# Two attention layers on one core: when normalizations start, how the divisors travel, and where the division stands

## The chip, the core and the metric

The kernel runs on one core of a Trainium2 chip. A time is the device time of one execution in microseconds (us); lower is better. The core has five engines that each work through their own queue in order: PE (TensorE, matrix products into PSUM), DVE (VectorE), ACT (ScalarE), POOL (GpSimd) and SP (SyncE, which here only issues transfers). An engine that waits at the head of its queue holds up everything behind it.

## The reference

The input `x` is 4 images of 256 channels and 64 x 64 pixels, in float32. Two layers follow, each with a residual:

```
x = x + layer0(group_norm(x))
x = x + layer1(group_norm(x))

layer0: q = Wq x                              (8 heads of 32 channels, 4096 queries)
        k, v = convolutions 2x2, stride 2     (1024 keys and values)
        out = softmax((q k + q pos) / sqrt(32)) v
layer1: q, k, v = 1x1 convolutions
        attention within each of 4 areas of 1024 pixels
        out = W_proj (attention + depthwise convolution 7x7 of v)
```

A group norm takes the mean and the variance over 8 channels and all pixels of an image, so its scale is known only when the whole image has been seen. Everything is computed in float32.

## The kernel before

**Units.** The attention of both layers and four images makes 128 units: 4 heads and 512 queries against 1024 keys. A unit has 8 steps, one for each 128 keys. Layer 0 of all four images comes first (`A`, batches 0 to 3), then layer 1 (`B`).

**Phases.** A main loop (L1157) runs 683 phases, each of one and a half steps. In a phase PE computes scores for three PSUM banks (`scores`, L430, products at L423), ACT takes three exponentials of them, 128 x 1024 each (L464 and L475, tile `p` or, in the first step of a unit, `acc`), PE multiplies the exponentials of the phase before by the values (`weighted`, L489, into the bank `av`), and DVE adds the exponentials up in `acc` (`add_up`, L499). The loop writes the order of every engine's queue by hand; nothing is reordered later.

**Side work.** Everything else is fitted into the phases. `at(g, j, f)` runs `f` after step `j` of unit `g`. `task_at` puts generator tasks (projections, convolutions) into the queue `side`; each phase takes 0, 1, 2 or, when late, 4 parts of it, if the task's `ready` allows. Only one PSUM bank is there for side work (`ps_side`). A phase does one of three things (L1181 to L1209): a unit's divisors, an entry of the queue `quick`, or parts of `side`.

**Normalization.** `plan_norm` (L331) plans three pieces for each image and layer: `aggregate` (DVE), then `means` and `variances`, both put into `quick`. `means` multiplies by the group matrix on PE (L347), copies on ACT (L348) and lets DVE form the deviation (L349 to L351); `variances` multiplies again (L355), ACT adds epsilon (L356), POOL takes the power -1/2 (L359) and forms the shift (L363, L364). Only then `norms[key]` is set. `later` (L282) queues the normalizations themselves (ACT, L387, on the loaded tiles `taps`, `hq`, `h`, `hv`), each with the earliest phase at which it may run: some phases after its load was issued. `norm_next` (L290) takes the first that is due at the end of a phase. `normalize` (L378) has a way out when the scale isn't there:

```
while key not in norms:
    while begun():
        advance()
    quick.popleft()()
```

**Division.** When a unit's sums are complete, `divisors` (L501) lets PE sum `acc` over the keys by products with ones (L508, bank `den`), and `divide` (L513) does the rest. Each head's 512 divisors stand in 32 equal partitions of `den`. ACT copies them to `den_sb` (L522). POOL sends 4 rows of it to the DRAM tile `rows` (L523) and from there, spread over 128 partitions as 128 x 16, into `few` (L524). A unit later DVE takes reciprocals of that small tile and sums for a check (`reciprocals`, L530, L531), POOL sends them to the DRAM tile `recs` (L532) and by four broadcasts into `rb` (L534, 32 partitions each, one buffer). Some steps later `multiply` (L537) on DVE multiplies `av_sb` by `rb` into `att`. `av_sb` is ACT's copy of the bank `av` (`evict`, L1118, L1124) and has two buffers. Steps of the two, for unit `g`:

```
at(*((g + 2, 1) if g < len(units) - 2 else (g + 1, 6)), reciprocals)
at(g + 2, 6 if g < len(units) - 2 else 0, multiply)
```

**What reads the result.** The residual of a chunk is added at (u + 2c + 4, 1) after its two units (L670, L813); the tile `att` has one buffer.

Of the kernel before, what the change touches and what calls it, by code (L numbers as in the profile page):

```python
# [9 lines left out]
FP = mybir.dt.float32  # L10
# [5 lines left out]
P = 128  # L16
# [44 lines left out]
def direct_path(  # L61
# [127 lines left out]

    side, quick = deque(), deque()
    now, last = [-1], len(BLOCKS) * UNITS * NKT

    phase = [0]
# [76 lines left out]
    def begun():  # L272
        return bool(side) and side[0][2]

    norms_left, norm_done = [], {}

    copies, behind = [0], [0.0]

# [10 lines left out]

    def norm_next(token=None):  # L290
        for n, (of, f, start) in enumerate(norms_left):
            if (of == token) if token else start <= phase[0]:
                del norms_left[n]
                f()
                norm_done[of] = phase[0]
                return True
        return False
# [33 lines left out]
    def plan_norm(key, g, j):  # L331

        name = f"{key[0]}{key[1]}"
        made = {}

        def aggregate():
            for tag, cols in (("mv", 2), ("gmean", 1), ("dev", 1), ("gvar", 1)):
                shape = [P, CT, cols] if cols > 1 else [P, CT]
                made[tag] = pool.tile(shape, FP, tag=tag, name=f"{tag}_{name}", bufs=2)
            mv = made["mv"]  # L340
            for t in range(CT):
                V.bn_aggr(out=mv[:, t, :], in_=stats[key][:, t].rearrange("p c s -> p (c s)"))

        def means():
            mv, mean, dev = made["mv"], made["gmean"], made["dev"]
            ps = ps_side(f"gm_{name}")[:, :CT]
            T.matmul(ps, lhsT=gmat, rhs=mv[:, :, 0], start=True, stop=True)  # L347
            S.copy(mean, ps)  # L348
            V.tensor_sub(dev, mv[:, :, 0], mean)  # L349
            V.tensor_mul(dev, dev, dev)  # L350
            V.tensor_add(dev, dev, mv[:, :, 1])  # L351

        def variances():
            ps = ps_side(f"gv_{name}")[:, :CT]
            T.matmul(ps, lhsT=gmat, rhs=made["dev"], start=True, stop=True)  # L355
            S.activation(made["gvar"], ps, AF.Identity, bias=eps)  # L356
            norm = pool.tile([P, 2, CT], FP, tag="norm", name=f"norm_{name}", bufs=8)
            shift, rstd = norm[:, 0, :], norm[:, 1, :]
            G.tensor_tensor(rstd, made["gvar"], neghalf, ALU.pow)  # L359
            if key == ("A", 0):  # L360
                V.scalar_tensor_tensor(shift, made["gmean"], -1.0, rstd, ALU.mult, ALU.mult)
            else:
                G.tensor_tensor(shift, made["gmean"], rstd, ALU.mult)  # L363
                G.tensor_scalar(shift, shift, -1.0, None, ALU.mult)  # L364
            norms[key] = shift, rstd

        def quietly(f, n):
            f()
            if key == ("A", 0):
                keep_busy(n)  # L370

        if key == ("A", 0):
            at(g - 1, 0, lambda: keep_busy(44))
        at(g, j, aggregate)
        at(g, j + 1, lambda: soon(lambda: quietly(means, 4)))
        at(g, j + (6 if g >= 0 else 3), lambda: soon(lambda: quietly(variances, 10)))
# [136 lines left out]
    def divide(g, unit):  # L513

        if g == len(units) - 1:

            V.tensor_mul(unit[4]()[:, unit[0], :], avs.pop(g), spare[1])  # L517
            return
        den_sb = pool.tile([P, CH], FP, tag="cout", name="den_sb", bufs=2)
        few = pool.tile([P, 2, CH // HD], FP, tag="few", name="few", bufs=2)  # L520
        rows = dram.tile([4, CH], FP, tag="rows", name=f"rows_{g}", bufs=4)
        S.copy(den_sb, dens.pop(g))  # L522
        G.dma_start(rows, den_sb[0:P:HD, :])  # L523
        G.dma_start(few[:, 0, :], rows.rearrange("h (q n) -> (h q) n", n=CH // HD))  # L524
        made = {}

        def reciprocals():
            rb = made["rb"] = pool.tile([P, CH], FP, tag="rb", name="rb", bufs=1)
            recs = dram.tile([4, CH], FP, tag="recs", name=f"recs_{g}", bufs=4)
            V.reciprocal(few[:, 1, :], few[:, 0, :])  # L530
            V.tensor_reduce(sums[:, :, g], few, AX.X, ALU.add)  # L531
            G.dma_start(recs.rearrange("h (q n) -> (h q) n", n=CH // HD), few[:, 1, :])  # L532
            for h in range(4):
                G.dma_start(rb[HD * h : HD * h + HD, :], recs[h : h + 1, :].to_broadcast([HD, CH]))  # L534

        def multiply():
            V.tensor_mul(unit[4]()[:, unit[0], :], avs.pop(g), made["rb"])  # L537

        at(*((g + 2, 1) if g < len(units) - 2 else (g + 1, 6)), reciprocals)
        at(g + 2, 6 if g < len(units) - 2 else 0, multiply)  # L540

    def att_of(key):
        if key not in atts:
# [4 lines left out]
    def plan_a(b, u, prep):  # L548
# [78 lines left out]
        for a in range(NAREA):  # L627
            g = prep + (1 + 3.6 * a if b == 1 else 0.05 + 3.7 * a if b else 6 + 2.2 * a)
            at(0, int(NKT * (g - 2.4)), lambda a=a: load(a))
            for n in range(8):  # L630
                at(0, (max(int(NKT * (g - 1.9)), 3) if b else int(NKT * (g - 1.6))) + n, lambda a=a, n=n: later(("taps", b, a), lambda: make_taps(a, n), fetched["a", a] + 4))
            for n in range(2):
                if b == 0 and a and n:
                    held.append((4, make_k, a, n))
                else:
                    task_at(int(NKT * (g + 0.6 * n)), 4, make_k, a, n, due=min(g + 3.7, u) if a < 3 or not n else u + 0.3, ready=normed("taps", b, a))
                task_at(
                    int(NKT * (g + 0.6 * n + 1.2)), 4, make_v, a, n, due=min(g + 4.2, u - 0.2), ready=normed("taps", b, a)
                )
# [38 lines left out]
        for c in range(NCH):  # L678
            g = u + 2 * c
            at(g - 3, 4, lambda c=c: fetch(c))  # L680
            for t in range(CT):
                at(g - 2, 1 + 2 * t, lambda c=c, t=t: later(
                    ("hq", b, c), lambda: norm_chunk(c, t), fetched["q", c] + 5, True
                ))
            for qd in range(2):
                task_at(NKT * (g - 2) + 4, 2, make_q, c, qd, due=g - 0.3, ready=normed("hq", b, c))
            at(g + 3, 0, lambda c=c: load_residual(c))
            at(g + 4, 1, lambda c=c: add_residual(c))
            at(g + 4, 2, lambda c=c: store_chunk(c))
# [12 lines left out]
    def plan_b(b, u):  # L702
# [67 lines left out]
        for a in range(NAREA):  # L770
            g = u + 4 * a
            at(g - 6, 3, lambda a=a: load(a))
            for t in range(CT):
                at(g - 5, 2 + 3 * t, lambda a=a, t=t: later(("hs", b, a), lambda: norm(a, t), since[a] + 6, True))
            for n in range(4):
                task_at(
                    NKT * (g - 4) + 1 + 4 * n, 2, make_k, a, n // 2, n % 2, due=g - 0.4, ready=normed("hs", b, a)
                )
            for n in range(4):
                at(g - 4, 3 + 2 * n, lambda a=a, n=n: load_v(a, n))  # L780
                at(g - 2, 1 + 2 * n, lambda a=a, n=n: make_v(a, n))
# [161 lines left out]
    def plan_values(b, c, start):  # L943
# [46 lines left out]
        when = int(start * NKT)  # L990
        at(0, when - 5, load)
        for t in range(CT):
            at(0, when + 5 + t, lambda t=t: later(("hv", b, c), lambda: norm(t), made["at"] + 6, True))
        for t in range(CT):
            task_at(
                when + 7, 2, values, t, due=start + 4,
# [160 lines left out]
    while f < PHASES or before or plan or side or quick or norms_left or to_add or to_divide:  # L1157
# [27 lines left out]
        elif due and not begun():  # L1185
            done_den = 1
            copies[0] += 1
            g = to_divide.popleft()
            divisors(g, *([last - 1] if g == final else []))
            if g < final:  # L1190
                divide(g, units[g])
            else:
                rb = pool.tile([P, CH], FP, tag="p", name="rb", bufs=PB)
                V.reciprocal(rb, dens[g])  # L1194
                spare.extend((dens.pop(g), rb))
        elif quick and not begun() and not cut and f < PHASES:
            quick.popleft()()
        else:
            if rate > 2:
                parts = side_parts(4)  # L1200
            elif rate > 1.5 or due or f >= PHASES or wanted >= (0.8 if cut else 1.5):
                parts = side_parts(2)
            elif begun() and side[0][0] % 2:
                parts = side_parts(1)
            elif boundary(mine):
                parts = side_parts(2) if wanted >= 0.9 else 0
            elif wanted >= 0.5 and not cut or begun():
                parts = side_parts(1)
            credit = max(-0.5, min(wanted - parts, 0.5))  # L1209
# [620 lines left out]
```

## Time and profile before

| what | us |
|---|---|
| median of 3 runs | 3091.56 (3090.89 to 3096.43) |
| the profiled execution | 3092.91 |
| its span, from the first to the last instruction | 3090.8 |
| VectorE busy in sums of exponentials (L499) | 2113.9, 1790 of 1218 ns |
| ScalarE busy in exponentials of 128 x 1024 (L464, L475) | 2033.8, 2048 of about 1.03 us |
| POOL issuing transfers of divisors (L523, L524, L532, L534) | 467.7 |
| mean granted TensorE clock | 0.996 |

Times in the profile belong to the one profiled execution. "Busy" is time in which an instruction runs on the engine; a line of the waits view has who waited, for whom, the total in us, how many times, and the longest. A line of a timeline has start, duration, engine, line of the code, operation, tile written and tiles read, shape, count of merged instructions and, in brackets, how long the engine stood idle before it and what ended that. A line of the windows view has a stretch of time and its length, then for each engine its busy time, and at the end the granted TensorE clock, the share of the DMA engines and GB/s.

### The profile page before, as it was taken

The numbers are of one execution on the slowest core, as the hardware profiler recorded it, in microseconds if no ns is written. First come the engines' busy times: TensorE is split into PE (matmuls) and PEld (weight loads), VectorE is DVE, ScalarE is ACT, GpSimd is POOL, SyncE is SP. The second block draws the span as 40 slices with busy tenths as digits, with TensorE's granted clock in tenths as the row PEclk, the third lists the DMA queues.
The fourth block names the chain that finished last, engine by engine and source line by source line (L and its number), as shares of the span: only waits on it lengthen the run. The fifth ranks groups of instructions, "written<-read, shape, count | busy, mean of one in ns | idle before, by whom it ended". The sixth has DMA issues, their size and how long they took to land. (4 is left out here: it accounts for less than half of the span.)

```text
span 3090.8 us, 108514 instructions
## 1 busy us (share of the span) xinstructions
PE 3036.6 (98%) x47254; PEld 1282.2 (41%) x47254; DVE 2516.2 (81%) x2721; ACT 2455.2 (79%) x2988; POOL 483.1 (16%) x921
## 2 busy tenths in 40 slices
PE   9999999999999999999999999999999999999998
PEld 6444333444444444334444444443444444443332
DVE  3788977789887787777888888777888888888888
ACT  3888877888888888788888887777777787788885
POOL 0111111111211111111112111111111111111111
PEclk9999999999999999999999999999999999999999
DMA  5244433566334556777865667667655565542222
GB/s 189 60 100 116 98 80 76 112 147 155 92 99 135 143 151 143 183 184 197 207 171 149 162 172 196 165 170 181 174 153 144 150 163 148 150 106 75 54 68 65
DMA packets 648316, 423.61 MB, mean 137 GB/s; under 512 B 411772, under 2 KB 556636, under 8 KB 647832
## 3 DMA queue, kind: packets, MB, share of 16 engines
q1 hardware_dynamic: 619384, 380.11, 48.6%
q0 software_dynamic: 28448, 36.48, 4.7%
q8 instruction: 373, 6.11, 0.8%
q14 instruction: 111, 0.91, 0.1%
HBM read 318.32 MB, written 98.09 MB: 135 GB/s over the span
## 5 line engine op out<-in xcount | busy, mean ns | idle before, releaser
L499 DVE TENSOR_TENSOR acc<-acc,p 128x1024 f32<-128x1024 f32 x1790 | 2113.9, 1218 | 424.9 <-PE av L489 313.6
L464 ACT ACTIVATE p<-s 128x1024 f32<-128x1024 f32 x1194 | 1159.4, 1025 | 416.5 <-PE s L423 406.0
L475 ACT ACTIVATE p<-s 128x1024 f32<-128x1024 f32 x598 | 619.6, 1036 | 0.3 <-DVE acc L499 0.2
L423 PE MATMUL s<-q,k_A 32*64 32x256 f32 (+1 forms) x10928 | 543.5, 497 | 17.1 <-ACT p L464 16.2
L423 PE MATMUL s<-q,k_B 32*64 32x512 f32 (+1 forms) x10912 | 537.8, 494 | 2.8 <-ACT p L464 2.0
L489 PE MATMUL av<-p,v_B 128*32 128x512 f32 (+1 forms) x4776 | 450.6, 487 | 0.0
L489 PE MATMUL av<-p,v_A 128*32 128x256 f32 (+1 forms) x4784 | 449.9, 486 | 0.0
L423 PEld LDWEIGHTS s<-q,k_A 32*64 32x64 f32 x10928 | 266.3, 131 | 342.6 <-ACT p L464 73.3
L423 PEld LDWEIGHTS s<-q,k_B 32*64 32x64 f32 x10912 | 267.2, 130 | 325.6 <-PE s L423 60.8
L534 POOL DMA_DIRECT2D rb<-recs x508 | 252.0, 502 | 526.7 <-DMA recs<-few 441.1
L532 POOL DMA_DIRECT2D recs<-few x127 | 70.0, 551 | 1407.6 <-DVE sums L531 1248.3
L489 PEld LDWEIGHTS av<-p,v_B 128*32 128x32 f32 x4776 | 149.3, 110 | 264.1 <-issue 238.2
L489 PEld LDWEIGHTS av<-p,v_A 128*32 128x32 f32 x4784 | 149.0, 110 | 228.9 <-issue 187.2
L464 ACT ACTIVATE acc<-s 128x1024 f32<-128x1024 f32 x172 | 167.0, 1023 | 82.1 <-PE s L423 81.9
L508 PE MATMUL den<-acc,ones 128*32 128x512 f32 x1024 | 140.8, 608 | 5.1 <-DVE acc L499 4.3
L524 POOL DMA_DIRECT2D few<-rows x127 | 71.2, 561 | 458.0 <-DMA rows<-den_sb 452.9
L167 PE MATMUL ops<-cv,wp_sb 128*32 128x512 f32 x1024 | 125.1, 598 | 6.1 <-DVE xm L828 3.2
L167 PE MATMUL k1ps<-h,wqkv_sb 128*32 128x512 f32 x1024 | 123.8, 598 | 2.7 <-ACT k_B L730 2.0
L167 PE MATMUL q0ps<-hq,wq_sb 128*32 128x512 f32 x1024 | 124.0, 598 | 1.4 <-ACT q L661 1.4
L167 PE MATMUL q1ps<-h,wqkv_sb 128*32 128x512 f32 x1024 | 124.3, 598 | 0.0
L167 PE MATMUL vals_ps<-hv,wqkv_sb 128*32 128x512 f32 x1024 | 124.1, 598 | 0.0
L167 PE MATMUL v0ps<-wkv,taps 128*32 128x256 f32 x2048 | 124.0, 386 | 0.0
(103 smaller groups left out, 2150.3 us busy)
## 6 DMA issues: line engine op xcount, KB each, us to landing
rows<-vals SPq DMA_DIRECT2D x384, 195.9 KB
rb<-recs POOLq DMA_DIRECT2D x508, 64.0 KB, 3.3
share<-vals SPq DMA_DIRECT2D x128, 195.9 KB
vala<-vout SPq DMA_DIRECT2D x128, 144.0 KB
vals<-vout SPq DMA_DIRECT2D x128, 144.0 KB
vc<-vala SPq DMA_DIRECT2D x64, 288.0 KB
band<-mats SPq DMA_DIRECT2D x96, 176.0 KB
hq<-in_x SPq DMA_DIRECT2D x32, 512.0 KB
```

Source lines behind the costliest of these rows:

```text
L167: T.matmul(out[cols, :], lhsT=lhsT[:, cols], rhs=rhs, start=start, stop=stop)
L423: T.matmul(out[n : n + WIDE], lhsT=unit[2]()[rows, unit[0], j * P + n : j * P + n + WIDE], rhs=unit[1]()[rows, cols], start=True, stop=True,)
L464: S.activation(p, (a, b)[n], AF.Exp, scale=SCALE)
L475: S.activation(p, c.rearrange("p b (l n) -> p b l n", l=2), AF.Exp, scale=SCALE)
L489: T.matmul(out, lhsT=v[:, j, unit[0] * P + HD * h : unit[0] * P + HD * h + HD], rhs=rhs, start=(j == 0 and not u), stop=(j == NKT - 1), sk ...
L499: V.tensor_add(to, to, p)
L508: T.matmul(dens[g][HD * h : HD * h + HD, :], lhsT=ones, rhs=p(h), start=(n == 0), stop=(n == len(sets) - 1),)
L524: G.dma_start(few[:, 0, :], rows.rearrange("h (q n) -> (h q) n", n=CH // HD))
L532: G.dma_start(recs.rearrange("h (q n) -> (h q) n", n=CH // HD), few[:, 1, :])
L534: G.dma_start(rb[HD * h : HD * h + HD, :], recs[h : h + 1, :].to_broadcast([HD, CH]))
```

## The change

Four things are edited. A normalization may start at the later of its old earliest phase and four phases after the phase in which `variances` of its key was placed (`known`, `after`). Two entries of `quick` are at least three phases apart. The divisors go from `den_sb` to `few` by one transfer inside SBUF; the DRAM tile `rows` is gone. The reciprocals stand one step earlier, at step 0 of unit g + 2, and the multiplication one step later, at step 7, except in the last units.

```diff
-    side, quick = deque(), deque()
+    side, quick, quick_at = deque(), deque(), [-9]
...
-    norms_left, norm_done = [], {}
+    norms_left, norm_done, known = [], {}, {}
+
+    def after(key, start):
+
+        return lambda: max(start, known.get(key, 1 << 20) + 4)
...
-            if (of == token) if token else start <= phase[0]:
+            if (of == token) if token else (start() if callable(start) else start) <= phase[0]:
...
             norms[key] = shift, rstd
+            known[key] = phase[0] if now[0] >= 0 else -4
...
-        rows = dram.tile([4, CH], FP, tag="rows", name=f"rows_{g}", bufs=4)
         S.copy(den_sb, dens.pop(g))
-        G.dma_start(rows, den_sb[0:P:HD, :])
-        G.dma_start(few[:, 0, :], rows.rearrange("h (q n) -> (h q) n", n=CH // HD))
+        G.dma_start(few[:, 0, :], den_sb[0:P:HD, :].rearrange("h (q n) -> h q n", n=CH // HD))
...
-        at(*((g + 2, 1) if g < len(units) - 2 else (g + 1, 6)), reciprocals)
-        at(g + 2, 6 if g < len(units) - 2 else 0, multiply)
+        at(*((g + 2, 0) if g < len(units) - 2 else (g + 1, 6)), reciprocals)
+        at(g + 2, 7 if g < len(units) - 6 else 6 if g < len(units) - 2 else 0, multiply)
...
-        elif quick and not begun() and not cut and f < PHASES:
+        elif quick and not begun() and not cut and f < PHASES and f > quick_at[0] + 2:
             quick.popleft()()
+            quick_at[0] = f
```

The start of all four kinds of normalization is wrapped in `after`: that of `taps` from `fetched["a", a] + 4` to `after(key, fetched["a", a] + 4)`, and in the same way those of `hq` (+ 5), `h` (+ 6) and `hv` (+ 6).

More of the change, by code (lines that the diff above doesn't have):

```diff
@@ L630, in plan_a @@
             for n in range(8):
-                at(0, (max(int(NKT * (g - 1.9)), 3) if b else int(NKT * (g - 1.6))) + n, lambda a=a, n=n: later(("taps", b, a), lambda: make_taps(a, n), fetched["a", a] + 4))
+                at(0, (max(int(NKT * (g - 1.9)), 3) if b else int(NKT * (g - 1.6))) + n, lambda a=a, n=n: later(("taps", b, a), lambda: make_taps(a, n), after(key, fetched["a", a] + 4)))
             for n in range(2):
@@ L682, in plan_a @@
                 at(g - 2, 1 + 2 * t, lambda c=c, t=t: later(
-                    ("hq", b, c), lambda: norm_chunk(c, t), fetched["q", c] + 5, True
+                    ("hq", b, c), lambda: norm_chunk(c, t), after(key, fetched["q", c] + 5), True
                 ))
@@ L773, in plan_b @@
             for t in range(CT):
-                at(g - 5, 2 + 3 * t, lambda a=a, t=t: later(("hs", b, a), lambda: norm(a, t), since[a] + 6, True))
+                at(g - 5, 2 + 3 * t, lambda a=a, t=t: later(("hs", b, a), lambda: norm(a, t), after(key, since[a] + 6), True))
             for n in range(4):
@@ L992, in plan_values @@
         for t in range(CT):
-            at(0, when + 5 + t, lambda t=t: later(("hv", b, c), lambda: norm(t), made["at"] + 6, True))
+            at(0, when + 5 + t, lambda t=t: later(("hv", b, c), lambda: norm(t), after(("B", b), made["at"] + 6), True))
         for t in range(CT):
```

## The prediction

> **What bounds the kernel now.** I read the page's busy times first, then the waits in total, then the timelines of the engines around TensorE's longest gaps.
>
> ```profile
> PE 3036.6 (98%) x47254; PEld 1282.2 (41%) x47254; DVE 2516.2 (81%) x2721; ACT 2455.2 (79%) x2988; POOL 483.1 (16%) x921
> ```
>
> TensorE is busy for 98% of the span, so the engine itself can give back at most 3090.8 - 3036.6 = 54.2 us of idle time, plus any time in which it is busy but slow. The other engines have slack. The change leaves every matmul in place, so the question is which gaps go. The waits in total:
>
> ```profile
> ACT taps L387 <- POOL norm_A L364: 6.9, 1, 6.9
> ACT hv L387 <- POOL norm_B L364: 6.1, 1, 6.1
> DVE att_B L537 <- DMA rb<-recs: 22.0, 13, 4.0
> DVE att_A L537 <- DMA rb<-recs: 15.9, 8, 3.2
> ```
>
> Two single waits of ScalarE for a normalization's scale, and 21 waits of VectorE for the broadcast reciprocals. The chain runs from POOL to TensorE. POOL's timeline, then ScalarE's, then TensorE's, at the first of the two:
>
> ```profile
> 393.45 1.98 POOL L534 DMA_DIRECT2D rb<-recs  x4 [4.38 <-DMA recs<-few]
> 395.42 0.58 POOL L523 DMA_DIRECT2D rows<-den_sb  x1
> 398.34 0.57 POOL L524 DMA_DIRECT2D few<-rows  x1 [2.34 <-DMA rows<-den_sb]
> 398.93 0.74 POOL L359 TENSOR_TENSOR norm_A<-gvar_A,neghalf 128x2 f32<-128x2 f32 x1
> ```
>
> ```profile
> 400.29 0.61 ACT L387 ACTIVATE taps<-xa,norm_A 128x256 f32<-128x256 f32 x1 [6.93 <-POOL norm_A L364]
> ```
>
> ```profile
> 402.78 2.90 PE L423 MATMUL s<-q,k_A 32*64 32x256 f32 x32 [5.95 <-ACT p L464]
> ...
> 410.08 1.55 PE L423 MATMUL s<-q,k_A 32*64 32x256 f32 x32
> ```
>
> The scale (`pow`, L359) stands in POOL's queue behind six DMA issues and two landings; the normalization stands at the head of ScalarE's queue; the exponentials stand behind it; TensorE has no free score bank for 5.95 us. Then the same 32 score products take 2.90 us instead of 1.55. The windows view says why (the number after POOL is the granted clock):
>
> ```profile
> 402.80:408.30 5.50, 5.50 (x60) 2.36 (x64) 4.60 (x5) 4.98 (x7) 0.00 (x0) 0.50 0.44 102
> 410.00:424.00 14.00, 14.00 (x224) 5.90 (x224) 7.32 (x9) 11.37 (x15) 3.25 (x6) 1.00 0.24 43
> 2422.20:2425.50 3.30, 3.30 (x14) 1.10 (x16) 1.19 (x3) 0.71 (x2) 0.58 (x2) 0.50 0.01 3
> ```
>
> After the gap the clock is half. The last line is another place: VectorE waited for `rb`, was late with a unit's sums, and the divisor products (L508) waited for them. VectorE's and TensorE's timelines of the longest such case and of the one with the halved clock:
>
> ```profile
> 2125.36 0.69 DVE L537 TENSOR_TENSOR att_B<-av_sb,rb 128x512 f32<-128x512 f32 x1 [3.90 <-DMA rb<-recs]
> ...
> 2414.62 0.69 DVE L537 TENSOR_TENSOR att_B<-av_sb,rb 128x512 f32<-128x512 f32 x1 [2.95 <-DMA rb<-recs]
> ```
>
> ```profile
> 2132.79 0.59 PE L508 MATMUL den<-acc,ones 128*32 128x512 f32 x1 [2.17 <-DVE acc L499]
> ...
> 2422.05 2.11 PE L508 MATMUL den<-acc,ones 128*32 128x512 f32 x5 [2.10 <-DVE acc L499]
> ```
>
> [...] it halves after 2.10 us at 2420 as well, and not after 2.17 us at 2130: a short gap may or may not cost the second half. [...] Here the gap between issuing `rows` and issuing `few`, one landing, was 1.4 to 7.7 us, median 3.1. [...]
>
> **How I price gaps.** I measure TensorE from the start of one phase's first score product to the next. Phases of one content have almost one length (their medians): 16 weighted products alone 3.17 us, with a unit's divisors or one side part 3.76 (8 first-layer value parts 3.77), with two parts 4.62 or 4.63. What exceeds this is a loss, slow clock included.
>
> **Part 1: the scale four phases old, group means apart.** In before, a normalization that was due while its scale was not yet known called the pending variances on the spot. In the changed program's instruction order the variance product stands in a phase of its own, `pow` stands directly behind one DMA issue, and the first normalization follows four phases later (about 4 x 4.5 = 18 us, where POOL needs under 7). What goes:
> - Batch 1 of the first layer: phases from 388.11, 393.00 and 402.78 last 4.88, 9.78 and 7.30 us against 3.76, 3.77 and 4.63: 1.12 + 6.01 + 2.67 = 9.80; the moved variance costs 0.05 elsewhere (3.22 against 3.17). Gain 9.75.
> - Second layer, batch 0: phases from 505.70, 511.07 and 520.18 last 5.37, 9.12 and 6.63 against 4.62, 3.77 and 4.63: 0.75 + 5.35 + 2.00 = 8.10, less 0.05. Gain 8.05.
> - Second layer, batch 1: the variance came one phase after the mean and waited 0.72 us for VectorE (phase from 895.95: 4.39 against 3.22). It now comes three phases after: gain 1.17.
> The waits of a mean for its aggregate (1.07 us at 495 and at 1634) are untouched. What it costs: the side work is packed differently until about 900 us. Counting phases by content in both orders and multiplying by the medians above, it is 0.7 us more, mostly two more phases with four parts (6.36 + 3.17 against twice 4.63). In one place four normalizations stand directly before the four-part key phase that reads them; they take 4 x 0.65 us of ScalarE against 1.5 us of scores: about 1 us of new wait. The bound there is 0 to 3.
>
> **Part 2: divisors in one transfer.** 127 issues of 0.56 us and 452.9 us of waits leave POOL's queue, and one HBM hop leaves the chain. Neither is on TensorE's path; by itself it is worth 0. It only moves `few` earlier: the new transfer is issued where `rows` was. VectorE's reciprocals move up by one or two sums in 84 units. Their new place is still at least 6.1 us after that issue, and at least 2.65 us after the time at which `rows` alone landed, so a transfer of the old first hop's length is hidden. The 64-byte pieces inside SBUF are not in the trace; if they took 3 us more, a few units would wait under 1 us on VectorE, which has 19% slack. I take 0; bound -1 to +4 us.
>
> **Part 3: multiplication a step later.** In 81 of 127 units the multiplication moves back behind three more sums, one phase; in 46 both steps fall into the same phase and nothing moves. Between reciprocals and multiplication stand 13 sums instead of 8 to 10 (45 units keep 10). All waits for `rb` over 0.2 us but the last (1.69 at 3071, in the tail, not moved) are in moved units; the longest, 3.99, is shorter than three sums of 1.2 us plus the earlier reciprocals. So these waits go, and with them the late divisors they caused: phases from 1123.33, 2129.08 and 2418.40 last 4.96, 7.03 and 8.19 against 3.76: 1.20 + 3.27 + 4.43 = gain 8.90. The other waits for `rb` (about 26 us) ended on VectorE alone. What is next: ScalarE's copy of the unit after next into `av_sb` (two buffers) must wait for this multiplication, with the exponentials behind it. Before, it started 2.7 to 13.8 us after the multiplication ended; for the moved units, with the multiplication put after the third sum, the slack is 4.0 us in the median, under 0.5 us in five, negative (-0.44) only at 2125, where the 3.90 us wait goes. I take 0; bound 0 to 3 us.
>
> **Sum.** 9.75 + 8.05 + 1.17 + 8.90 - 0.7 - 1.0 = 26.2 us. The profiled execution took 3092.9 us (2.1 outside the span), giving 3066.7; the median of the runs is 1.3 us lower, 3091.56, giving 3065.4. I say 3066.
>
> **Rivals.**
> - *Only the scale stalls go.* The late divisors come back from other VectorE load (at 2899 a phase lost 0.67 us with no wait for `rb`), or short `av_sb` waits eat that gain: 3091.6 - 17 = 3074. For: VectorE is 81% busy, and reciprocals now precede up to two last sums of the unit before. Against: the three large cases each follow a wait for `rb`.
> - *More goes.* Some 24 phases are 0.46 us too long behind a busy ScalarE or VectorE; if half of these 11 us went, 3060. Nothing in the diff aims there.
> - *Nothing goes*, since POOL's queue still holds the scale longer than four phases: 3091. Against: only one DMA issue stands ahead of it now.
> - *Slower: ScalarE's copy waits for the multiplication* at L1124. It decides once VectorE runs over 4 us later than I projected in most moved units. At 5 us late, 81 units would wait about 1 us each; with half covered by ScalarE's slack, 40 us lost against 26 won plus one or two halved clocks: 3107. Against: median slack 4.0 us.
>
> **Chances.** My forecast 0.60, only the scale stalls 0.25, more 0.05, nothing 0.04, slower 0.06. The likely cases lie from 3061 to 3078, with the bounds of the unknown costs. Under 0.2% (6 us) a measurement of this kernel cannot tell a change: faster 0.90, same 0.04, slower 0.06.
>
> **What would show it.** Right: no ScalarE wait for `norm` near 400 or 515; the half-clock windows there and at 2422 gone, the one at 1224 (products waiting for convolution rows) perhaps still there; waits for `rb` near 2 us in total; no `rows`; TensorE's idle time near 35 us. Wrong: waits of L1124's copy for `att`, of the reciprocals for `few`, or new gaps before L508.

## The result, and the profile after

| | before | after |
|---|---|---|
| median | 3091.56 (3089.84 to 3096.43, 5 runs) | 3075.54 (3073.27 to 3079.41, 5 runs) |
| ratio after to before, 95% interval | | 0.9946 (0.9932 to 0.9961) |
| profiled execution, its span | 3092.91, 3090.8 | 3073.27, 3071.1 |
| TensorE idle within the span | 54.2 | 35.2 |

The change gains 16.0 us where 26.2 were forecast. The two kernels were measured side by side twice more: the gain was 16.0 and 23.0 us (ratios 0.9945 and 0.9927). Between the two profiles it is 19.6.

The page's busy times of the changed kernel. As before, TensorE is the bound. In this profile 19.0 of the 19.6 us by which the span is shorter are idle time that went (54.2 - 35.2). Its busy time is almost the same, but time at half clock counts as busy in full (402.80 to 408.30 in before: 5.50 us busy of 5.50, at a granted clock of 0.50); where the half clock went is told below.

```profile
PE 3035.9 (99%) x47254; PEld 1281.1 (42%) x47254; DVE 2519.9 (82%) x2721; ACT 2456.4 (80%) x2988; POOL 433.1 (14%) x794
```

The waits in total of the changed kernel (who waited, for whom, us in all, times, longest):

```profile
POOL few L527 <- ACT den_sb L526: 288.1, 82, 36.7
...
DVE st_A L565 <- DMA xs<-in_x: 11.1, 4, 4.4
...
ACT vout L973 <- DMA vals<-vout: 5.6, 2, 3.7
...
DVE att_B L540 <- DMA rb<-recs: 1.4, 1, 1.4
```

The two waits of ScalarE for a scale (6.9 and 6.1 us) are no longer in the list, and of 37.9 us of waits for `rb` one of 1.4 is left. POOL no longer waits for `rows` (452.9 us in all before); instead its wait for ScalarE's copy of the divisors has grown from 110.4 to 288.1 us. Two lines have grown, and both matter below: `st_A` on the load of `xs` (before 7.8 us in all), and `vout` on the store out of its own buffer (before 2.9, but 7.6 in e5, a second profile of before).

POOL's timeline of the changed kernel at the first place, then ScalarE's:

```profile
396.21 0.70 POOL L527 DMA_DIRECT2D few<-den_sb  x1 [3.83 <-ACT den_sb L526]
399.44 1.46 POOL L363 TENSOR_TENSOR norm_A<-gvar_A,neghalf 128x2 f32<-128x2 f32 x1 [2.52 <-ACT gvar_A L360]
400.98 0.72 POOL L367 TENSOR_TENSOR norm_A<-gmean_A,norm_A 128x2 f32<-128x2 f32 x1
401.80 1.07 POOL L368 TENSOR_SCALAR norm_A<-norm_A 128x2 f32<-128x2 f32 x1
```

```profile
419.62 1.18 ACT L392 ACTIVATE taps<-xa,norm_A 128x256 f32<-128x256 f32 x2
...
424.24 0.66 ACT L392 ACTIVATE taps<-xa,norm_A 128x256 f32<-128x256 f32 x1
...
429.96 2.18 ACT L392 ACTIVATE taps<-xa,norm_A 128x256 f32<-128x256 f32 x4
```

The power now waits only for its input, 2.52 us; one DMA issue stands before it. The scale is ready at 402.87 and the first normalization with it starts at 419.62, without a wait in brackets. The windows view of the changed kernel over the two scale stalls, the two late divisors and two new places (the third number from the end is the granted clock):

```profile
387.10:402.60 15.50, 15.50 (x256) 6.43 (x240) 12.60 (x15) 12.74 (x16) 6.24 (x9) 1.00 0.34 77
502.00:512.40 10.40, 10.40 (x150) 3.83 (x138) 9.07 (x10) 10.09 (x14) 3.26 (x6) 1.00 0.40 102
2121.00:2124.50 3.50, 3.50 (x56) 1.29 (x52) 2.92 (x3) 3.13 (x5) 0.00 (x0) 1.00 0.79 201
2403.00:2408.00 5.00, 5.00 (x78) 2.19 (x67) 3.22 (x6) 5.00 (x7) 0.55 (x1) 1.00 0.22 36
1401.00:1408.00 7.00, 5.70 (x100) 3.87 (x104) 4.66 (x8) 5.91 (x8) 0.55 (x1) 0.76 0.53 98
17.00:24.00 7.00, 6.75 (x40) 5.65 (x43) 2.02 (x8) 3.74 (x9) 0.72 (x1) 0.52 1.10 333
```

At the four old places TensorE is busy throughout at full clock. But about 17 us after the start, and at 1401, there is half clock that the profile of before does not have.

I cut both traces into phases, as in the prediction, and took the difference of the time from the first phase of a stretch to the first of the next. In us, rounded, negative is a gain; the last three columns are other profiles of the same changed kernel (experiments e10, e1 and e6):

| place (time in before) | forecast | after | e10 | e1 | e6 |
|---|---|---|---|---|---|
| 318 to 472, first scale stall | -9.75 | -8.2 | -8.2 | -8.2 | -8.2 |
| 472 to 639, second | -8.05 | -8.2 | -8.2 | -8.2 | -8.2 |
| 639 to 896, side work packed differently | +1.7 (whole kernel) | +3.6 | +3.8 | +2.5 | +4.0 |
| 896 to 1070, late variance | -1.17 | -0.35 | -0.35 | -0.35 | -0.35 |
| divisors at 1123, 2129, 2418 | -8.90 | -8.8 | -8.8 | -8.8 | -8.8 |
| all else | 0 | +2.4 | +1.4 | -0.4 | -0.8 |
| sum | -26.2 | -19.6 | -20.3 | -23.5 | -22.3 |

Every named stall went, at nearly the size forecast. What failed is the packing; outside the steps, time was lost in two profiles and not in the other two. The experiments ask which part brings what, whether the remainder belongs to the change, and whether the parts add up.

### The profile page after: what moved, and what is told of

Same layout as the page of the kernel before. It is cut to its first block, busy times and chain, and to the rows that moved or that the text cites. A ratio compares the mean times of both kernels' runs of the same rounds, so it can differ in the third digit from the quotient of the medians.

```text
span 3071.1 us, 108308 instructions
## 1 busy us (share of the span) xinstructions
PE 3035.9 (99%) x47254; PEld 1281.1 (42%) x47254; DVE 2519.9 (82%) x2721; ACT 2456.4 (80%) x2988; POOL 433.1 (14%) x794
## 4 chain that ended last, share of the span: by engine, by line
PE 89%; DMA 3%; DVE 3%; ACT 2%; issue 2%; SPq 1%; POOL 0%; DVEq 0%; ACTq 0%; POOLq 0%
PE s L428 30%; PE av L494 26%; PE conv_ps L1048 4%; PE q1ps L167 4%; PE k1ps L167 4%; PE den L513 4%; PE k0ps L167 4%; PE v0ps L167 4%; PE q0ps L167 4%; PE ops L167 4%; PE vals_ps L167 3%; DVE acc L504 2%; DMA vals<-vout 1%; ACT p L469 1%; DMA rows<-vals 1%
## 5 line engine op out<-in xcount | busy, mean ns | idle before, releaser
L527 POOL DMA_DIRECT2D few<-den_sb x127 | 90.7, 714 | 288.4 <-ACT den_sb L526 288.1
L167 PE MATMUL k0ps<-taps,wkv 128*32 128x256 f32 x2048 | 123.9, 383 | 0.0
```

The lines of the kernel that those rows point to most:

```text
L167: T.matmul(out[cols, :], lhsT=lhsT[:, cols], rhs=rhs, start=start, stop=stop)
L527: G.dma_start(few[:, 0, :], den_sb[0:P:HD, :].rearrange("h (q n) -> h q n", n=CH // HD))
```

## Experiments

"Part 1" is the scale four phases old with the group means apart, "part 2" the single transfer, "part 3" the moved reciprocals and multiplication. Medians and ratios:

| run | kernel | median (range, runs) | before beside it | ratio (95%) |
|---|---|---|---|---|
| e1 | changed kernel again | 3077.88 (3069.31 to 3080.81, 6) | 3093.87 | 0.9945 (0.9933 to 0.9958) |
| e2 | part 1 alone | 3083.52 (3080.18 to 3089.04, 6) | 3093.87 | 0.9963 (0.9951 to 0.9975) |
| e3 | parts 2 and 3 | 3079.30 (3074.07 to 3085.16, 6) | 3093.87 | 0.9950 (0.9937 to 0.9963) |
| e4 | part 2 alone | 3092.23 (3087.17 to 3097.99, 14) | 3093.87 | 0.9994 (0.9986 to 1.0002) |
| e7 | part 3 alone | 3086.23 (3079.24 to 3092.65, 10) | 3096.52 | 0.9969 (0.9960 to 0.9979) |
| e8 | multiplication alone a step later | 3086.42 (3085.04 to 3088.73, 7) | 3096.52 | 0.9969 (0.9958 to 0.9980) |
| e9 | parts 1 and 3 | 3076.61 (3074.81 to 3079.16, 5) | 3094.90 | 0.9941 (0.9927 to 0.9954) |
| e10 | changed kernel again | 3071.88 (3070.93 to 3072.80, 5) | 3094.90 | 0.9927 (0.9913 to 0.9941) |
| e11 | changed kernel, means a step later | 3083.96 (3081.07 to 3088.28, 6) | 3094.90 | 0.9970 (0.9958 to 0.9982) |

e1 to e4 ran on one chip, e5 to e8 on another, e9 to e11 on a third. e5 and e6 are one profile each, of the kernel before (3099.51) and of the changed one (3070.49).

### Part 1 alone, and parts 2 and 3 without it (e1, e2, e3)

e1 is the changed kernel. e2 has its diff without this; e3 is the kernel before with only this:

```diff
-        rows = dram.tile([4, CH], FP, tag="rows", name=f"rows_{g}", bufs=4)
-        G.dma_start(rows, den_sb[0:P:HD, :])
-        G.dma_start(few[:, 0, :], rows.rearrange("h (q n) -> (h q) n", n=CH // HD))
+        G.dma_start(few[:, 0, :], den_sb[0:P:HD, :].rearrange("h (q n) -> h q n", n=CH // HD))
...
-        at(*((g + 2, 1) if g < len(units) - 2 else (g + 1, 6)), reciprocals)
-        at(g + 2, 6 if g < len(units) - 2 else 0, multiply)
+        at(*((g + 2, 0) if g < len(units) - 2 else (g + 1, 6)), reciprocals)
+        at(g + 2, 7 if g < len(units) - 6 else 6 if g < len(units) - 2 else 0, multiply)
```

Expected of e1:

> The changed kernel once more, for a second profile of it. If the half-clock stretch of 6.8 us at 17 us (3.3 us lost in the head, whose instructions the change does not touch) and the wait of 2.15 us before the convolution at 1400 us are chance, they will be absent or elsewhere here, and the span without them is near 3065 us. If they belong to the changed order, they stand at the same places. Time either way 3073 to 3079 us.

In e1 the half clock near 17 us stands again, 3.4 us long; at 1400 TensorE waited 1.21 us and the clock stayed full.

Expected of e2:

> Part 1 alone (normalizations held until the scale is four phases old, group means apart); two transfers for the divisors, reciprocals at step 1, multiplication at step 6 as before. My theory (parts add, part 1 worth 19 us less the repacking of side work): no wait of ScalarE for norm, no half clock near 400 and 515, but about 20 waits for rb with some 35 us in total, late divisors near 2120 and 2410, and 3076 to 3082 us. Rival (the stalls at the divisors are replaced by others, so part 1 is the whole gain): same time as the full change, 3074 to 3077 us.

Expected of e3:

> Parts 2 and 3 without part 1: one transfer inside SBUF, reciprocals at step 0, multiplication at step 7; normalizations as in before. My theory: waits for rb down to 1 to 3 us, no late divisors at 1123, 2129 and 2418, but ScalarE waits about 7 and 6 us for norm near 400 and 515 with half clock after each, and about 3083 us (8.9 us gained). Rival (only the scale stalls count): 3089 to 3092 us.

e2 gained 10.4 us (less than expected), e3 14.6 (more), and both together (e1) 16.0: the parts do not add up. e3 has no delayed normalization, so its scale stalls should have stayed whole. Its waits in total:

```profile
ACT vout L968 <- DMA vals<-vout: 10.8, 4, 5.8
...
ACT hv L387 <- POOL norm_B L364: 3.2, 1, 3.2
...
ACT taps L387 <- POOL norm_A L364: 2.6, 1, 2.6
...
DVE att_B L535 <- DMA rb<-recs: 1.7, 1, 1.7
```

The scale waits are 2.6 and 3.2 us instead of 6.9 and 6.1. POOL's timeline of e3 at the first place says why:

```profile
389.19 1.98 POOL L532 DMA_DIRECT2D rb<-recs  x4 [1.42 <-DMA recs<-few]
395.02 0.70 POOL L522 DMA_DIRECT2D few<-den_sb  x1 [3.84 <-ACT den_sb L521]
395.73 0.74 POOL L359 TENSOR_TENSOR norm_A<-gvar_A,neghalf 128x2 f32<-128x2 f32 x1
```

The power still stands behind the divisors' transfers. But reciprocals a step earlier let `recs` and `rb` leave POOL earlier, and one hop less spares it the 2.34 us of waiting for `rows`. Of the 16.4 us that the changed kernel takes from the two stretches of the scale, parts 2 and 3 alone take 9.3 (6.5 and 2.8 in the phases). So the parts overlap: each of them pulls the scale out from behind the divisors.

e2 shows the other side. It loses 7.5 us between 639 and 896, more than the changed kernel (the wait for `xs` described below is 5.5 us long here, with half clock after it), and keeps 36.9 us of waits for `rb`.

### The single transfer alone (e4), with a second look at both kernels (e5, e6)

e4 is the kernel before with only the first part of the diff above.

> Part 2 alone: the divisors by one transfer inside SBUF, every step of reciprocals and multiplication as in before. My theory: the reciprocals do not stand earlier, so rb does not come earlier; waits for rb stay near 38 us in 15 to 25 waits, late divisors stay, 3089 to 3093 us. Rival (the shorter path of the divisors is what takes the waits for rb away): waits for rb under 5 us and about 3083 us.

1.6 us in the medians, and an interval that holds no change. Its waits in total show `rb` as late as before, and the second scale too; the wait for the first is 1.5 us shorter (5.4 instead of 6.9), and the stretch around it 2.5 us:

```profile
DVE att_A L535 <- DMA rb<-recs: 23.3, 12, 5.1
...
DVE att_B L535 <- DMA rb<-recs: 19.9, 10, 4.1
...
ACT hv L387 <- POOL norm_B L364: 6.2, 1, 6.2
ACT taps L387 <- POOL norm_A L364: 5.4, 1, 5.4
```

e5 and e6 ask what is chance.

> The kernel before, once more, for a second profile of it: how much of a profile is chance. If the 3 us lost in the head by every kernel but before is chance, this profile loses them too. The two waits for norm (7 and 6 us) and the half clock after them should stand at 400 and 517 us again; the places of the shorter half-clock stretches may differ. 3089 to 3097 us.

> The changed kernel, a third profile. Its two profiles so far were taken from the fastest runs of their sets (3073.3 and 3069.3 us, medians 3075.5 and 3077.9). Theory (the shortfall against the forecast is chance losses that the fast profiles lack): a slower run than these shows, at otherwise equal phases, more half-clock stretches or longer waits of ScalarE for the store of vout near 1400 us, worth the difference. Rival (a steady loss the accounting missed): equal phases are longer everywhere.

e5 has both scale waits again (7.2 and 6.1 us) and 50.4 us of waits for `rb`, so these belong to the kernel. Its span is 6.7 us longer than that of the first profile of before, 3.5 of them near 1400 us, where the changed kernel lost 2.6: that place is slow in both kernels at times. e6 lost only 0.2 there. At 3070.49 us it is not the slower run that its theory speaks of, so that theory stays untested.

### Steps moved, and the multiplication alone (e7, e8)

e7 is the kernel before with both new steps and the two old transfers; e8 with only the multiplication moved.

```diff
-        at(g + 2, 6 if g < len(units) - 2 else 0, multiply)
+        at(g + 2, 7 if g < len(units) - 6 else 6 if g < len(units) - 2 else 0, multiply)
```

> Part 3 alone: reciprocals a step earlier, multiplication a step later, the divisors still by two transfers through DRAM. Theory (the steps take the waits for rb away; the single transfer matters only for POOL's queue): waits for rb under 5 us in total; the waits for norm shorter than 6.9 and 6.1 us (POOL's earlier transfers are issued a step earlier) but longer than the 2.6 and 3.2 of parts 2 and 3 together; 3080 to 3084 us. Rival (the single transfer is needed for it): waits for rb over 15 us, time over 3087 us.

> The multiplication a step later, and nothing else. Theory: the waits for rb go (the longest was 4.0 us, the move is three sums of 1.2 us in 81 units) but for one or two short ones, while POOL's queue stays as in before, so the waits for norm stay near 7 and 6 us with a half clock after each; 3081 to 3086 us. If the waits for norm shrink here too, the explanation by POOL's queue is wrong.

They gain 10.3 and 10.1 us, so the earlier reciprocals bring no time here by themselves, although e7's waits for the scale shrink to 5.4 and 4.0 us, as expected: the earlier issues do thin POOL's queue. The waits in total of e8:

```profile
ACT taps L387 <- POOL norm_A L364: 7.1, 1, 7.1
...
ACT hv L387 <- POOL norm_B L364: 6.0, 1, 6.0
...
DVE att_B L537 <- DMA rb<-recs: 3.1, 3, 1.4
...
DVE att_A L537 <- DMA rb<-recs: 0.8, 2, 0.6
```

`rb` falls from 37.9 to 3.9 us with this one line of code, while the scale stays as late as it was: moving the multiplication is enough to take nine tenths of the waits for `rb` away. The late divisors go with them, 1.2, 2.5 and 4.3 us in the phases.

### The changed kernel without the single transfer (e9), beside the changed kernel (e10)

e9 is the changed kernel with the two transfers through `rows` put back.

> The changed kernel with the two transfers of before (DRAM tile `rows`) put back; steps and normalizations as changed. Forecast's theory (the single transfer is worth nothing once the scales are four phases old): the same time as the changed kernel, ratio to before 0.993 to 0.996, less than 2 us from the changed kernel beside it apart from chance; no ScalarE wait for norm, rb waits about 2 us, POOL busy again 483 us, and at most a few VectorE waits for `few` under 1 us each, as two landings (about 3.4 + 3.0 us and 0.6 us of issue) end near the reciprocals' new place. Rival (the single transfer has a share of its own in the gain, as parts 2 and 3 together gave 14.6 us against 10.3 for part 3 alone): about 4 us slower than the changed kernel, with waits for norm or for few to show it.

> The changed kernel again, beside the other two on the same chip. Ratio to before 0.994 to 0.996 as twice before. If the half-clock stretches fall by chance, they stand elsewhere than in the three profiles so far, except at about 17 us and in the tail; if the place at 1400 us (vout waiting for its buffer's store) is systematic, it stands again.

e9 is 4.7 us slower than e10 in the medians, and the two ranges do not touch: here the transfer that gained nothing clear alone seems to have a share. Its waits in total, and then the timelines of VectorE and TensorE in e9 around the longest of the new waits:

```profile
DVE few L535 <- DMA few<-rows: 20.2, 9, 5.2
```

```profile
1589.67 0.69 DVE L542 TENSOR_TENSOR att_A<-av_sb,rb 128x512 f32<-128x512 f32 x1
1595.54 0.25 DVE L535 RECIPROCAL few<-few 128x16 f32<-128x16 f32 x1 [5.18 <-DMA few<-rows]
```

```profile
1597.29 1.67 PE L513 MATMUL den<-acc,ones 128*32 128x512 f32 x5 [1.50 <-DVE acc L504]
```

Two landings are too slow for VectorE here: it waits nine times for `few`, at 1595 for 5.18 us, the sums behind it come late and so do the divisor products, and 2.6 us of the span are lost there. In none of the four profiles of the changed kernel is a wait of VectorE for `few` left; e7 and e8, which also have two transfers, have 9.4 and 5.5 us of it. So the single transfer is what takes these waits away. How much time it is worth is not settled. 3.3 us of the difference between the two profiles lie near 655 to 662, where ScalarE waited 3.45 us for the load of `xa`, the input of `taps`; e6 and e11, which have the single transfer, waited 1.8 and 1.9 us there, so I cannot say that the second transfer delayed it. And the ratio of e9 to before (0.9941) is no worse than that of the changed kernel in its first two sets (0.9946 and 0.9945); only the set beside it was faster.

e10 is the fastest set of runs and has no half clock at the start. e9 has none there either; the other profiles of changed or half changed kernels have, and the two of before have not. As the changed kernel has it in one profile and not in another, the change does not force it. The gap ahead of it is in before too: TensorE waits 2.00 us there, 1.93 in the first profile of the changed kernel and 1.78 in e10. What the traces show of it stands in the last section.

### The group means a step later (e11)

An attempt at a better version: the deviation's products wait 1.07 us for VectorE's aggregate at two places.

```diff
-        at(g, j + 1, lambda: soon(lambda: quietly(means, 4)))
+        at(g, j + (2 if g >= 0 else 1), lambda: soon(lambda: quietly(means, 4)))
```

> The changed kernel with the group means asked for one step later than the aggregate's own end (step j + 2 for g at least 0), so that the deviation's product does not wait for VectorE's aggregate (1.07 us at about 490, 1245 and 1622 us in both kernels). If these waits cost their length: 1 to 3 us faster than the changed kernel, and the three waits gone; too little for the ratio to tell. Rival: the side work is packed differently in some 100 phases again, which costs 2 to 4 us as it did in the stretch from 700 to 900 us: no gain or up to 3 us slower.

Both waits went, and the stretch from 472 to 639 gained 2.4 us more than in the changed kernel. Yet the kernel is 12.1 us slower than e10 beside it. The side parts after each mean shifted, in some 100 phases. VectorE's and the DMA issuer's timelines in e11 at the largest single loss:

```profile
2094.28 1.21 DVE L816 SCALAR_TENSOR_TENSOR cv<-cv,bpe_sb,att_B 128x512 f32<-128x512 f32 x1
2104.25 1.14 DVE L816 SCALAR_TENSOR_TENSOR cv<-cv,bpe_sb,att_B 128x512 f32<-128x512 f32 x1 [8.77 <-DMA cv<-conv]
```

```profile
2088.91 0.40 SPq L1029 DMA_DIRECT2D band<-mats  x1
2089.36 4.37 SPq L1032 DMA_DIRECT2D rows<-vals  x4
2094.43 7.29 SPq L804 DMA_DIRECT2D cv<-conv  x8
```

The second of the two tiles is loaded by eight issues that end at 2101.7; VectorE stood at the sum that needs it from 2095.5. In e10 the last of these loads is issued at 2089.6, and the sums of both chunks follow each other without a wait. The 8.77 us cost TensorE 7.6, half clock included. The rival, that repacking eats such a gain, held, and its price was forecast too low.

## Why the prediction was right, and where it was not

- **The bound.** Right: idle time went from 54.2 to 35.2, against "near 35" (34.0 to 37.6 in the four profiles). Part of the gain should also have shown as shorter busy time: at the named places half clock stood for 6.8, 6.8 and 3.4 us, an estimated loss of 8.5 us, half of that (the granted clock was 0.50, and 32 score products took 2.90 us instead of 1.55). It is gone from there, yet busy time only went from 3036.6 to 3035.9, in part because half clock came elsewhere, at the start above all (6.8 us). By the same estimate, half clock cost 11.7 and 11.5 us in the two profiles of before and 8.0, 2.4, 5.0 and 4.9 in after, e1, e6 and e10.
- **Part 1, the stalls.** Right in mechanism and size: 16.4 us in the two stretches, in every profile of the changed kernel, where 17.80 were forecast, the repacking inside these stretches included. Neither of the two waits for a scale is left, and the clock is full there.
- **The named new wait.** It did not come: after the four normalizations at 429.96 TensorE lost 0.19 us, not 1.0.
- **The packing, 0.7 and the wait's 1.0 us.** This is the term that was too small. I counted phases by content and multiplied by medians, as if a phase cost the same wherever its side work stands. Per place, the packing took back 1.4 us of the first two stretches, 2.5 to 4.0 between 639 and 896, and 0.8 at the late variance: 4.7 to 6.2 instead of 1.7. The count itself held: by these medians, the phases from 318 to 1070 hold 0.9 us more work, against 0.8 forecast with the two moved variances. What failed is what was left out, phases that last longer than their content: besides the named stalls, they sum to 5.3 us in before and to 9.2 to 10.7 in the four profiles of the changed kernel. The largest piece shows in VectorE's and ScalarE's timelines of the changed kernel:

```profile
705.35 1.29 DVE L565 BATCH_NORM_STATS2 st_A<-xs 128x6 f32<-128x512 f32 x2 [4.37 <-DMA xs<-in_x]
706.55 3.67 DVE L504 TENSOR_TENSOR acc<-acc,p 128x1024 f32<-128x1024 f32 x3
```

```profile
707.85 2.16 ACT L469 ACTIVATE p<-s 128x1024 f32<-128x1024 f32 x2 [2.10 <-DVE acc L504]
...
726.82 2.16 ACT L469 ACTIVATE p<-s 128x1024 f32<-128x1024 f32 x2 [2.10 <-DVE acc L504]
```

The statistics wait for a load that was issued at 700.23, 5 us before; the sums behind them come late, ScalarE waits for a buffer of exponentials that VectorE has not read, and four phases of TensorE lose 2.7 us together (3.0 in e10, 1.6 in e1), where before none of them lost 0.1. Why the load is late is read from the DMA queue's own waits: a load of this kind (L108) needs a chunk buffer that a projection on TensorE has read, and the queue waited for that 32.4 us in before (23.9 for `q0ps`, 8.5 for `vals_ps`) and 53.0 in the changed kernel (27.3 and 25.7); delayed normalizations would delay these projections. One of these waits, 20.2 us for `vals_ps` from 551.6, is new. It is not a wait of the late load itself, but the loads behind it have less room: the late load of `xs` and the five before it were issued 5.0 to 10.8 us before their use, the same six in before 6.0 to 21.1. That the delayed normalizations are the cause is not shown; I did not try it by itself.

- **Part 2, "by itself it is worth 0".** Right by itself (e4), and the working held: the transfer landed in 3.8 us in the median, where `rows` and `few` took 3.4 and 3.0 one after the other, and no reciprocal waits for it. But the sentence hides that it keeps waits away from the other parts: without it the changed kernel has 20.2 us of waits for `few` and was 4.7 us slower on the one chip where it was tried. I had written that the new place of the reciprocals is covered for one landing, and did not ask what two would do.
- **Part 3.** Right: 8.90 forecast, 8.8 in the phases; alone it gains 10.1 to 10.3. The rival that the late divisors come back did not happen, nor did ScalarE wait for the multiplication: in the moved units the slack of `av_sb` was 3.5 us in the median against 4.0 projected, and 0.22 at the least against -0.44.
- **What no step named.** Outside the steps the four profiles lost 2.4 and 1.4 us and gained 0.4 and 0.8. In the first profile that is 3.3 lost at the start and 2.6 near 1400, against 2.6 gained near 1200 to 1270 and 1.4 in the tail. At 1400 the chain is the same in the profiles of the changed kernel; ScalarE's timeline in the first, then TensorE's:

```profile
1401.54 0.71 ACT L973 ACTIVATE vout<-vals_ps,bqkv_sb 128x512 f32<-128x512 f32 x1 [3.72 <-DMA vals<-vout]
```

```profile
1402.30 1.33 PE L1048 MATMUL conv_ps<-share 88*32 88x128 f32 x32 [2.15 <-ACT vout L973]
1403.39 1.94 PE L1048 MATMUL conv_ps<-rows,band 88*32 88x128 f32 x32
```

`vout` waits for the store out of the buffer that it is about to write, and after 2.15 us of idling the clock is half. The stretch around it was 0.2 to 6.0 us longer than in the first profile of before in all twelve other profiles, 3.5 in e5, which is the kernel before: so it isn't the change's.

- **The forecast itself.** 3066 was 9.5 us too low, inside the range. The number alone is nearer to the rival that only the scale stalls go (3074); the profiles speak against that rival, since the late divisors went too. Of the 10.2 us between the forecast gain and the measured 16.0, 3.0 to 4.5 are the packing. The rest moves from set to set (gains 16.0, 16.0, 23.0), as the medians of before do (3091.56 to 3096.52); the second profile of before is 6.7 us longer than the one I summed against. Part of it is half clock, estimated above at 2.4 to 8.0 us in the four profiles of the changed kernel: the mean granted clock of before lay at 0.994 to 0.997 in its runs, of the changed kernel at 0.996 to 0.999. How much of the 16.0 or 23.0 is chance, the runs do not settle.

## What to carry to other kernels

Where an in-order queue carries both a short value that others wait for and a stream of transfers, look at what stands in front of the value: each change here that thinned the queue ahead of it took part of the same stall, so price such edits together and not as a sum. An edit that is worth nothing alone can keep waits away from its neighbour, so test it by taking it out of the full change too. When side work is placed by due times, moving it by one step costs through loads and buffers that come free later, which counting phases by content does not see: look at which loads the shifted work triggers and who stands behind their readers.

## What the runs showed of the hardware

- The length of the idling alone did not decide whether TensorE's clock was halved. It was halved with gaps of 5.95 and 5.29 us (up to 402.78 and 520.18 in before), and after 2.10 us (at 2420 in before) and 2.15 us (at 1402 in the changed kernel), not after 2.17 us (at 2130 in before). A stretch of half clock lasted 3.41 or 6.83 us, unless the end of the program cut it short. In each trace the beginnings of half clock lie on a grid. In before they are 401.50, 517.55, 1224.11 and 2422.19, the last three 34, 241 and 592 times 3.4133 us after the first; in the changed kernel 17.24, 1403.05, 3055.10 and 3068.76, the last three 406, 890 and 894 times 3.4133 us after the first. In each of the 13 profiles all beginnings lie on one such grid, within 6 ns, and where the grid lies changes from profile to profile. The windows view of before, cut at this grid around the gaps of 2.17 and 2.10 us (the first number after the length is TensorE's busy time, the third from the end the granted clock):

```profile
2128.64:2132.06 3.42, 1.98 (x40) 0.80 (x32) 3.39 (x4) 2.81 (x4) 0.00 (x0) 1.00 0.91 271
2132.06:2135.47 3.41, 2.66 (x18) 0.68 (x21) 2.07 (x4) 1.58 (x3) 0.55 (x1) 1.00 0.78 223
2418.78:2422.19 3.41, 1.31 (x33) 0.65 (x18) 3.38 (x5) 3.41 (x5) 0.00 (x0) 1.00 0.30 48
2422.19:2425.60 3.41, 3.41 (x14) 1.10 (x16) 1.20 (x3) 0.82 (x2) 0.68 (x2) 0.50 0.01 2
```

  The gap of 2.17 us is split by the grid into 1.44 and 0.73 us, and the clock stays full; that of 2.10 us falls into one stretch of the grid, and the next has half clock. So does that of 2.15 us in the changed kernel (1399.64 to 1403.05, 1.25 us busy; from there a granted clock of 0.50). In all profiles together, from 2 us after the start, a stretch of the grid at full clock with more than 2.05 us of TensorE idle was followed by half clock in 43 of 43 cases, one with under 1.5 us never, and one between in 17 of 46 (TensorE's busy time is modelled, so these limits are rough). At about 17 us, the stretch with the gap held 1.59 us of idle in before and 2.00 in the first profile of the changed kernel. So whether a gap of some 2 us cost half clock depended, at least in large part, on where the grid fell in these profiles. How much of the range of the changed kernel's runs, 3069.31 to 3080.81, comes from that was not shown.
- One transfer of 4 rows of 512 values to a 128 x 16 tile inside SBUF took POOL 0.72 us to issue (0.58 and 0.56 for the two through DRAM) and 3.8 us to land in the median, hardly more than the 3.4 us of one hop to DRAM. That hop's 127 transfers in before left 508 data packets of 2 KB, 4 each.
- POOL worked its queue in order: in before, ScalarE had written the input of the power at 393.36 (L356, 393.10 and 0.26 us long), but the power started at 398.93, directly behind DMA issues of which two had waited 4.38 and 2.34 us for landings.
